# Entry 0's scores ahead of its values, and the other entries' projections in pieces of four row tiles, in a two-layer graph attention kernel

## The chip, the cores and the metric

The kernel runs on one core of one Trainium2 chip. The metric is the device time of one execution in microseconds (us); lower is better. A core has TensorE (PE, matrix products into PSUM), VectorE (DVE), ScalarE (ACT), GpSimd (POOL), and SyncE (SP), which here only issues DMA transfers. Data on the chip lie in SBUF.

## The reference

Eight graphs ("entries", B = 8) of N = 2048 nodes with D = 256 features share one adjacency matrix. Layer 0 is an attention layer of H = 8 heads of 32 features, layer 1 one with dot products as scores. After each there is a residual and a layer norm.

```python
# layer 0
x_proj = einsum('bnd,hdf->bhnf', x, W)
e_src  = einsum('bhnf,hf->bhn', x_proj, a_src)
e_dst  = einsum('bhnf,hf->bhn', x_proj, a_dst)
e = leaky_relu(e_src[..., :, None] + e_dst[..., None, :], 0.2)
e = e + softplus(beta_tilde) * log(adj + 1e-6)
e = where(adj > 0, e, neg_inf)
h = einsum('bhij,bhjf->bhif', softmax(e), x_proj)
x = layernorm(x + concat_heads(h) @ W_out.T)
# layer 1
h1, h2, h3 = x @ W1, x @ W2, x @ W3
e = where(adj > 0, leaky_relu(h1 @ h2.T, 0.2), NEG_INF)
x = layernorm(x + relu(softmax(e) @ h3))
```

## The kernel before, in words

All arithmetic is fp32. Rows of N are cut into NT = 16 row tiles of 128, or into NB = 4 groups of four row tiles (512 rows). D is two halves of 128 (KC = 2).

Layer 0 of an entry has two parts. The **projection** (`project`) transposes x on PE a group at a time (`turn`, L252; `tr` into PSUM, copied by ACT to `xt`, L257). It then multiplies each row tile by `wp`, the 256 columns of W and, behind them, 16 columns that give both score vectors of the eight heads (L267). ACT copies the values to `v` (L269) and the scores to `both` (L270). After the last row tile come the factors: the maximum over the tiles on DVE (L276) and over the partitions on POOL (L277), `cs` and the shifted scores (L279, L281), two exponents into `re`, and one DVE instruction that scales all of `v` (L286). Entries 1 to 7 then store `v` and `re` in device memory (`v_d`, `re_d`, L289). At last PE transposes `cs` (`est`, L293) and its exponent goes to `c_d` (L296), from where `query_rows` (L308) later reads each head's row back into all 128 partitions, as `c`.

The **attention** (`step`) makes 64 steps: four passes over two heads each (`hp`), and in a pass 16 tiles of source nodes (`jt`). A step needs the tile `mt` of the transposed mask weights. For each of the two heads DVE computes `s = max(c, re) * mt` (L330, 128x2048), and PE multiplies s into the numerator `val` and the denominator `den` (L355, 16 instructions each). The denominators of some tiles don't go over PE one by one: for the tiles in `SUMMED` (L67), ACT makes a scaled copy `d` of the first (L343), DVE adds the others to it (L337), and PE takes up the sum once with a product by ones at the pass's end. `finish` copies `val` and `den` out of PSUM and takes the reciprocals through device memory (`rc`, `rec_d`, `rb`). After every second pass DVE multiplies `ht` by them (L383).

The first pass of entry 0 makes the mask as well: `make_m` loads a block of adj (L176) and computes `m` (DVE L178 and L181, ACT L179 and L180). `make_mt` transposes it on PE (`mtp`, L190), copies it by ACT (L191) and stores it (`mt_d`, L192). Later passes load `mt` (L197).

`output` (products `y`, L408, and the first layer norm), `turn` (L424) and `Dot` are layer 1. From entry 1 on, layer 0 of entry b is woven into layer 1 of entry b - 1.

What sets the order: PE runs its instructions in the order in which the program writes them (L86). The order of the other engines and of the DMA queue on SP is fixed when the kernel is built, by a planner that takes instructions by their place in the program and by its estimate of when they can start. Each engine and SP then runs its own list in order. A tile's buffer count (`bufs`) says how many of a tag can live at once: four `s`, three PSUM tiles of the tag `mm`, one x group `xg` (L166).

Entry 0 is projected whole before its first step. The projections of entries 1 to 7 are cut into pieces, one row tile each with two more per entry for the factors and the `est` (7 x 18 = 126), and these are spread evenly over the first 60 of entry 0's steps:

```python
    pieces = (B - 1) * (NT + 2)
    for k in range(NP * NT):
        gats[0].step()
        due = [min(i * pieces // (NP * NT - 4), pieces) for i in (k, k + 1)]
        for _ in range(due[1] - due[0]):
            next(others)
```

In a piece that begins a group, the turn of the group after it comes just behind that row tile, and takes its x from a load that was issued when the turn before it was done. `later_weights` prepares the weights of the later stages in five further pieces. Entry 1's `v`, like that of all later entries, comes back from device memory (`load`, L301) into the tag `v`, which entry 0's values hold until its last step. The hand-over runs two steps of entry 1, two groups of entry 0's output, one step, two groups, one step (L547).

Of the kernel before, what the change touches and what calls it, by code (L numbers as in the profile page):

```python
# [9 lines left out]
F32 = mybir.dt.float32  # L10
BF16 = mybir.dt.bfloat16
I32 = mybir.dt.int32
AF = mybir.ActivationFunctionType
# [5 lines left out]
P = 128  # L19
# [8 lines left out]
def kernel(  # L28
# [35 lines left out]
    NP = H // HP  # L64
    IG = BK // P

    SUMMED = [(1, 3, 6, 8, 11, 13), (1, 3, 6, 9, 12)] + [(1, 3, 6, 8, 11, 13)] * (B - 2)  # L67

    const = ctx.enter_context(tc.tile_pool(name="const", bufs=1))
    dram = ctx.enter_context(tc.tile_pool(name="dram", bufs=1, space=DRAM))  # L70
# [7 lines left out]
    def mm_tile(name):  # L78
        return ps.tile([P, BK], F32, tag="mm", name=name)
# [25 lines left out]
    beta_c = beta[:, 3:4]  # L105


    first_x = [wide.tile([P, NT // 2, D], F32, tag="p", name="xr", bufs=2) for _ in range(2)]
    for half, xr in enumerate(first_x):
        nc.sync.dma_start(xr, x[0].rearrange("(t p) d -> p t d", p=P)[:, ts(half, NT // 2), :])  # L110


    wp = const.tile([P, KC, D + 2 * H], F32)
    for kc in range(KC):
        nc.sync.dma_start(
# [3 lines left out]
    for a, dst in ((a_dst, wp[:, :, D:D + H]), (a_src, wp[:, :, D + H:])):  # L119
        a_bc = small.tile([P, D], F32, tag="row", name="a_bc", bufs=4)  # L120
        nc.sync.dma_start(a_bc, bass.AP(tensor=a.tensor, offset=a.offset, ap=[[0, P], [1, D]]))
        for kc in range(KC):
            wa = small.tile([P, D], F32, tag="row", name="wa", bufs=4)
            nc.vector.tensor_mul(wa, wp[:, kc, 0:D], a_bc)
            nc.vector.tensor_reduce(dst[:, kc, :], wa.rearrange("p (h f) -> p h f", h=H), AX.X, ALU.add)  # L125

    wot = const.tile([P, KC, D], F32)
    w12 = const.tile([P, KC, D], F32)
# [30 lines left out]
    rec_d = dram.tile([B, NP, 4, HALF], F32, name="rec_d")  # L159
    x1_d = dram.tile([B, N, D], F32, name="x1_d")  # L160

    def x_groups():

        for b in range(1, B):
            for g in range(NB):
                xg = wide.tile([P, IG, D], F32, tag="pen", name="xg", bufs=1)  # L166
                nc.sync.dma_start(xg, x[b].rearrange("(t p) d -> p t d", p=P)[:, ts(g, IG), :])
                yield xg

    groups = x_groups()  # L170
    ahead = []

    def make_m(jt):

# [9 lines left out]
    def make_mt(jt, m):  # L184

        mt = wide_tile("mt", "mt", 2)
        for g in range(NB):
            t = mm_tile("mtp")
            for k in range(IG):
                nc.tensor.transpose(t[:, ts(k, P)], m[:, g * IG + k, :], ident)  # L190
            nc.scalar.copy(mt[:, ts(g, BK)], t)  # L191
        nc.sync.dma_start(mt_d[ts(jt, P), :], mt)  # L192
        return mt
# [36 lines left out]
    class Gat:  # L230
# [4 lines left out]
            self.units = ((hp, jt) for hp in range(NP) for jt in range(NT))  # L235
            self.ms, self.mts = [], []

        def project(self):


            b = self.b
            kept = "v" if b == 0 else ("h3", "x1t")[b % 2]
            self.v = v = whole.tile([P, NT, D], F32, tag=kept, name="v")
            both = small.tile([P, NT, 2 * H], F32, name="both", bufs=1)
            xts = []

            def turn(g):
                if b == 0:
                    xr = first_x[g // 2][:, ds(g % 2 * IG, IG), :]
                else:  # L250
                    xr = ahead.pop() if ahead else next(groups)
                xt = chunk.tile([P, KC, BK], F32, tag="ht", name="xt", bufs=3)  # L252
                for kc in range(KC):
                    t = mm_tile("tr")
                    for k in range(IG):
                        nc.tensor.transpose(t[:, ts(k, P)], xr[:, k, ts(kc, P)], ident)
                    nc.scalar.copy(xt[:, kc, :], t)  # L257
                xts.append(xt)
                if b > 0:
                    ahead.extend(xg for xg in [next(groups, None)] if xg is not None)  # L260

            turn(0)
            for it in range(NT):
                g, k = divmod(it, IG)
                t = mm_tile("proj")
                for kc in range(KC):
                    nc.tensor.matmul(t[:, 0:D + 2 * H], xts[g][:, kc, ts(k, P)], wp[:, kc, :],  # L267
                                     start=(kc == 0), stop=(kc == KC - 1))
                nc.scalar.copy(v[:, it, :], t[:, 0:D])  # L269
                nc.scalar.copy(both[:, it, :], t[:, D:D + 2 * H])  # L270
                if k == 0 and g + 1 < NB:
                    turn(g + 1)
                yield
            top = small.tile([P, 2, H], F32, name="top", bufs=1)
            ed, es = both[:, :, 0:H], both[:, :, H:2 * H]
            nc.vector.tensor_reduce(top[:, 0, :], ed.rearrange("p t h -> p h t"), AX.X, ALU.max)  # L276
            nc.gpsimd.partition_all_reduce(top[:, 1, :], top[:, 0, :], P, bass_isa.ReduceOp.max)  # L277
            cs = small.tile([P, H, NT], F32, name="cs", bufs=1)
            nc.vector.tensor_tensor(cs, es.rearrange("p t h -> p h t"),  # L279
                                    top[:, 1, :].unsqueeze(2).to_broadcast([P, H, NT]), ALU.add)  # L280
            nc.vector.tensor_tensor(ed, ed, top[:, 1:2, :].to_broadcast([P, NT, H]), ALU.subtract)  # L281
            self.re = re = small.tile([P, 2, NT, H], F32, name="re", bufs=2)
            nc.scalar.activation(re[:, 0], ed, AF.Exp, scale=-(1.0 - ALPHA))
            nc.scalar.activation(re[:, 1], ed, AF.Exp)
            v4 = v.rearrange("p t (h f) -> p (t h) f", f=DH)
            nc.vector.tensor_tensor(v4, v4, re[:, 1].rearrange("p t h -> p (t h)").unsqueeze(2).to_broadcast(  # L286
                [P, NT * H, DH]), ALU.mult)
            if b > 0:
                nc.sync.dma_start(v_d[b], v)  # L289
                nc.sync.dma_start(re_d[b], re)  # L290
            yield
            t = mm_tile("est")
            nc.tensor.transpose(t[:, 0:P], cs.rearrange("p h t -> p (h t)"), ident)  # L293
            est = row_tile("est")[:, 0:P]
            nc.scalar.activation(est, t[:, 0:P], AF.Exp, scale=1.0 - ALPHA)
            nc.sync.dma_start(c_d[b].rearrange("h (t p) -> (h t) p", p=P), est)  # L296
            yield

        def load(self):
            self.v = whole.tile([P, NT, D], F32, name="v")  # L300
# [4 lines left out]
        def query_rows(self, h):  # L305
# [2 lines left out]
            nc.sync.dma_start(c, c_d[self.b, h:h + 1, :].to_broadcast([P, N]))  # L308
            return c

        def step(self, count=1):

            for _ in range(count):
# [3 lines left out]
                    self.val = pacc.tile([P, HALF], F32, tag="val", name="val")  # L317
                    self.den = pacc.tile([P, HALF], F32, tag="den", name="den")
                first = self.b == 0 and hp == 0
                while first and len(self.mts) < min(jt + 2, NT):  # L320
                    at = len(self.mts)
                    while len(self.ms) < min(at + 1 + (jt > 0), NT):
                        self.ms.append(make_m(len(self.ms)))
                    self.mts.append(make_mt(at, self.ms[at]))
                mt = self.mts[jt] if first else load_mt(jt, self.b == 0)
                s = []
                for a in range(HP):
# [3 lines left out]
                    s.append(sa)  # L331
                v, e = self.v, self.re[:, 1]
                heads = [hp * HP + a for a in range(HP)]
                chain = () if first else SUMMED[self.b]
                if jt - 1 in chain[1:]:
                    for d, sa, h in zip(self.sums, self.last, heads):
                        nc.vector.scalar_tensor_tensor(d, sa, e[:, jt - 1, h:h + 1], d, ALU.mult, ALU.add)  # L337
                self.last = s
                self.products(self.val, [v[:, jt, ts(h, DH)] for h in heads], s, jt == 0, jt == NT - 1)
                if jt in chain[:1]:  # L340
                    self.sums = [wide_tile("d", "d" if self.b else "p", 2) for _ in heads]
                    for d, sa, h in zip(self.sums, s, heads):
                        nc.scalar.activation(d, sa, AF.Copy, scale=e[:, jt, h:h + 1])  # L343
                if jt not in chain:
# [170 lines left out]


    gats = [Gat(b) for b in range(B)]
    for _ in gats[0].project():
        pass
    others = (1 for g in gats[1:] for _ in g.project())  # L520
    weights = later_weights()
    pieces = (B - 1) * (NT + 2)
    for k in range(NP * NT):
        gats[0].step()
        due = [min(i * pieces // (NP * NT - 4), pieces) for i in (k, k + 1)]
        for _ in range(due[1] - due[0]):
            next(others)
        if k >= NT and k % 4 == 2:
            next(weights, None)

    dot = None
    for b in range(1, B + 1):
        gat, fresh = gats[b - 1], gats[b] if b < B else None

        def layer_0(count):
            if fresh:
                fresh.step(count)

        if fresh:
            fresh.load()  # L540
        rows = gat.output()

        def output(count):
            for _ in range(count):
                next(rows)

        if dot is None:  # L547
            layer_0(2)
            for _ in range(2):
                output(2)  # L550
                layer_0(1)
        else:

            dot.step(lambda k: layer_0((0, 0, 2)[k]))
            dot.step(lambda k: (output((1, 1, 2)[k]), layer_0((0, 1, 1)[k])))
        for _ in gat.turn():
            layer_0(1)
        dot = Dot(gat)
        dot.step(lambda k: layer_0((2, 1, 1)[k]))
        for i in range(NT - 3):  # L560
            dot.step(lambda k: layer_0((0, 2 - (i % 3 == 2), 2)[k]))
# [33 lines left out]
```

## Time and profile before

| | |
|---|---|
| time, median of 3 runs | 4466.91 us (4461.9 to 4466.94) |
| the profiled execution | 4464.3 us, span 4462.5 us |
| PE busy | 4254.7 us (95%) |
| DVE busy | 3688.7 us (83%) |
| ACT busy | 1682.0 us (38%) |
| moved by DMA | 843.53 MB, 189 GB/s over the span |
| `s` (L330) on DVE | 1024 instructions, 2342 ns each |
| `d` (L337) on DVE | 302 instructions, 2344 ns each |

How to read it: the profile is of one execution, and all its times are from the start of the span. "Busy" is the time in which an engine had an instruction running. The ends of matrix products are modelled, so PE's busy time is an upper reading. A group line names the line of the kernel, engine, operation, output and inputs, count, busy time and mean, and then the idle time of that engine just before the group and what ended it. A line of waits names who waited for whom: us in total, how many times, the longest. A timeline row has start, length, engine, line, operation, tiles and count, and in brackets the idle time before it with what ended that.

### The profile page before, as it was taken

The numbers are of one execution on the slowest core, as the hardware profiler recorded it, in microseconds if no ns is written. First come the engines' busy times: TensorE is split into PE (matmuls) and PEld (weight loads), VectorE is DVE, ScalarE is ACT, GpSimd is POOL, SyncE is SP. The second block draws the span as 40 slices with busy tenths as digits, with TensorE's granted clock in tenths as the row PEclk, the third lists the DMA queues.
The fourth block names the chain that finished last, engine by engine and source line by source line (L and its number), as shares of the span: only waits on it lengthen the run. The fifth ranks groups of instructions, "written<-read, shape, count | busy, mean of one in ns | idle before, by whom it ended". The sixth has DMA issues, their size and how long they took to land.

```text
span 4462.5 us, 59194 instructions
## 1 busy us (share of the span) xinstructions
PE 4254.7 (95%) x24748; PEld 2217.8 (50%) x24748; DVE 3688.7 (83%) x2603; ACT 1682.0 (38%) x3041; POOL 13.4 (0%) x14
## 2 busy tenths in 40 slices
PE   6888889999999999999999999999999999999999
PEld 4444344444454454545455454545444454444666
DVE  5799988898899889898989889898889979898222
ACT  5622223333333333333233333333233343333455
POOL 0000000000000000000000000000000000000000
PEclk9999899999999999999999999999999999999999
DMA  7877666666555565555545565555555564554211
GB/s 211 265 251 258 221 212 214 219 221 239 183 182 179 187 216 181 194 186 201 198 167 191 190 213 187 186 193 192 187 180 199 184 217 175 193 181 144 72 50 41
DMA packets 251501, 843.53 MB, mean 189 GB/s; under 512 B 32352, under 2 KB 151136, under 8 KB 175712
## 3 DMA queue, kind: packets, MB, share of 16 engines
q1 hardware_dynamic: 215904, 806.17, 51.7%
q10 hardware_dynamic: 35328, 33.56, 2.2%
q8 instruction: 194, 3.18, 0.3%
q14 instruction: 75, 0.61, 0.0%
HBM read 763.76 MB, written 75.37 MB: 188 GB/s over the span
## 4 chain that ended last, share of the span: by engine, by line
PE 60%; DVE 14%; issue 7%; DMA 3%; ACT 2%; SPq 0%; ACTq 0%; DVEq 0%
PE acc L504 16%; PE e L469 15%; PE val L355 12%; DVE s L330 9%; PE den L355 8%; PE pt L488 4%; DVE d L337 4%; DMA mt<-mt_d 2%; PE y L408 2%; PE h1p L459 2%; PE h3p L439 1%; DVE p L474 0%; ACT p L475 0%; DMA rc<-dn 0%; DVE ht L410 0%
## 5 line engine op out<-in xcount | busy, mean ns | idle before, releaser
L330 DVE SCALAR_TENSOR_TENSOR s<-c,re,mt 128x2048 f32<-128x2048 f32 x1024 | 2354.2, 2342 | 178.8 <-PE den L355 117.7
L355 PE MATMUL val<-s,v 128*32 128x512 f32 x8192 | 1044.2, 611 | 83.3 <-DVE s L330 79.2
L504 PE MATMUL acc<-h,pts 128*128 128x256 f32 x4096 | 949.6, 380 | 2.0 <-ACT pts L490 1.2
L469 PE MATMUL e<-x1t,h 128*128 128x512 f32 x2048 | 906.1, 595 | 6.6 <-ACT h L461 6.5
L504 PEld LDWEIGHTS acc<-h,pts 128*128 128x128 f32 x4096 | 748.2, 190 | 92.2 <-ACT pts L490 6.3
L337 DVE SCALAR_TENSOR_TENSOR d<-s,re,d 128x2048 f32<-128x2048 f32 x302 | 701.7, 2344 | 0.0
L355 PE MATMUL den<-s,re 128*32 128x512 f32 x5280 | 677.6, 602 | 3.2 <-ACT dn L370 3.2
L469 PEld LDWEIGHTS e<-x1t,h 128*128 128x128 f32 x2048 | 379.1, 190 | 459.3 <-issue 416.3
L355 PEld LDWEIGHTS val<-s,v 128*32 128x32 f32 x8192 | 244.4, 111 | 698.2 <-issue 507.4
L490 ACT COPY pts<-pt 128x512 f32<-128x512 f32 x512 | 298.7, 584 | 766.3 <-PE pt L488 759.1
L471 ACT ACTIVATE p<-e 128x512 f32<-128x512 f32 x512 | 303.4, 596 | 434.7 <-PE e L469 431.1
L474 DVE CUSTOM_DVE_ANT_0 p<-p,pen 128x2048 f32<-128x2048 f32 x128 | 293.0, 2289 | 203.8 <-ACT p L471 203.0
L355 PEld LDWEIGHTS den<-s,re 128*32 128x32 f32 x5280 | 186.6, 112 | 413.7 <-issue 399.3
L488 PEld LDWEIGHTS pt<-ident,p 128*128 128x128 f32 x2048 | 238.9, 141 | 222.8 <-issue 159.4
L475 ACT ACTIVATE p<-p,neg 128x2048 f32<-128x2048 f32 x128 | 256.9, 2007 | 239.7 <-DVE neg L474 239.7
L488 PE MATMUL pt<-ident,p 128*128 128x128 f32 x2048 | 319.3, 279 | 6.2 <-ACT p L475 6.2
L511 ACT ACTIVATE z<-acc,rec 128x256 f32<-128x256 f32 x128 | 60.9, 476 | 369.6 <-PE acc L504 339.7
L512 DVE TENSOR_TENSOR z<-z,x1r 128x256 f32<-128x256 f32 x128 | 53.8, 420 | 159.6 <-ACT z L511 156.1
L267 PE MATMUL proj<-wp,xt 128*128 128x272 f32 x512 | 142.0, 419 | 11.8 <-DVE wp L125 8.0
L439 PE MATMUL h3p<-w3s,x1t 128*128 128x256 f32 x512 | 124.0, 386 | 17.1 <-ACT x1t L434 16.2
L343 ACT ACTIVATE d<-s,re 128x2048 f32<-128x2048 f32 x62 | 124.3, 2008 | 35.4 <-DVE ht L383 24.6
L408 PE MATMUL y<-wot,ht 128*128 128x256 f32 x512 | 119.4, 390 | 15.8 <-DVE ht L383 15.8
(82 smaller groups left out, 1886.9 us busy)
## 6 DMA issues: line engine op xcount, KB each, us to landing
mt<-mt_d SPq DMA_DIRECT2D x496, 1024.0 KB, 4.9
c<-c_d SPq DMA_DIRECT2D x64, 1024.0 KB, 7.1
pen<-pen_d SPq DMA_DIRECT2D x112, 512.0 KB, 3.4
xg<-in_x_dram SPq DMA_DIRECT2D x60, 512.0 KB, 5.1
adj_t<-in_adj_dram SPq DMA_DIRECT2D x16, 1024.0 KB, 7.2
mt_d<-mt SPq DMA_DIRECT2D x16, 1024.0 KB, 8.3
rb<-rec_d SPq DMA_DIRECT2D x64, 256.0 KB, 4.2
x_d<-ht ACTq DMA_DIRECT2D x32, 512.0 KB, 3.6
```

The source lines that it names most:

```text
L330: nc.vector.scalar_tensor_tensor(sa, self.cs[a], self.re[:, 0, jt, h:h + 1], mt, ALU.max, ALU.mult)
L337: nc.vector.scalar_tensor_tensor(d, sa, e[:, jt - 1, h:h + 1], d, ALU.mult, ALU.add)
L355: nc.tensor.matmul(dst[ts(q, DH), ts(c, BK)], weights[q % 2], s[q % 2][:, ds(q // 2 * HALF + c * BK, BK)], start=start, stop=stop)
L408: nc.tensor.matmul(y[:, i, :], self.ht[:, g * IG + k + i, kc, :], wot[:, kc, :], start=(kc == 0), stop=(kc == KC - 1))
L439: nc.tensor.matmul(t[:, ts(i, D)], x1t[:, kc, ts(2 * (j - 1) + i, P)], w3s[:, kc, :], start=(kc == 0), stop=(kc == KC - 1))
L469: nc.tensor.matmul(t, self.h1[:, kc, ts(it % IG, P)], self.x1t[:, kc, ts(c, BK)], start=(kc == 0), stop=(kc == KC - 1))
L471: nc.scalar.activation(p[:, ts(c, BK)], t, AF.Prelu, alpha=ALPHA)
L474: nc.vector.tensor_tensor_reduce(p, p, pen, -1.0, FMAX, ALU.add, ALU.min, neg)
L475: nc.scalar.activation(p, p, AF.Exp, bias=neg, scale=-1.0, accum_out=den)
L488: nc.tensor.transpose(t[:, ts(k, P)], p[:, ts(g * IG + k, P)], ident)
L490: nc.scalar.copy(pt, t)
L504: nc.tensor.matmul(acc, now[:, ts(k, P)], self.h3[:, j, :], start=(j == 0), stop=(j == NT - 1))
```

## The change

Entry 0's x is loaded in four pieces of four row tiles, issued behind the weights. All its groups are transposed first, into one tile `xt0`. Then 64 small PE instructions compute the scores of all 16 row tiles at once (16 columns each, into one PSUM tile), the factors follow, and only then the values are computed, without the score columns, group by group, with the scaling of `v` cut into four pieces. The `est` of entry 0 comes after the first group, its first `mt` after the second.

The other entries' projections come as 28 pieces of four row tiles (one group), one on each second step (k = 1, 3, ...). A piece transposes the x of the piece after it first and asks for the x of the one after that; then it computes its own four row tiles, scores included. The `est` of an entry comes behind the first row tiles of the next one. The entries come in the order 2 to 7, then 1. Their values lie alternately in the tags `v` and `h3`; entry 1's stay in `v` and are neither stored nor loaded again, and entry 0's own lie in the tag `x1t`. Entry 0 sends all denominators over PE. The hand-over runs three steps of entry 1, all four groups of output, one step.

```diff
-    SUMMED = [(1, 3, 6, 8, 11, 13), (1, 3, 6, 9, 12)] + [(1, 3, 6, 8, 11, 13)] * (B - 2)
+    SUMMED = [(), (1, 3, 6, 9, 12)] + [(1, 3, 6, 8, 11, 13)] * (B - 2)
...
-            kept = "v" if b == 0 else ("h3", "x1t")[b % 2]
-            both = small.tile([P, NT, 2 * H], F32, name="both", bufs=1)
+            self.both = small.tile([P, NT, 2 * H], F32, name="both", bufs=2)
...
+        def scores_first(self, xt):
+            t = mm_tile("both")
+            for it in range(NT):
                 for kc in range(KC):
+                    nc.tensor.matmul(t[:, ts(it, 2 * H)], xt[:, kc, ts(it, P)], wp[:, kc, D:],
+                                     start=(kc == 0), stop=(kc == KC - 1))
+            nc.scalar.copy(self.both.rearrange("p t h -> p (t h)"), t[:, 0:NT * 2 * H])
...
+        def scale(self, g):
+            v = self.v[:, ts(g, IG), :].rearrange("p t (h f) -> p (t h) f", f=DH)
+            e = self.re[:, 1, ts(g, IG), :].rearrange("p t h -> p (t h)")
+            nc.vector.tensor_tensor(v, v, e.unsqueeze(2).to_broadcast([P, IG * H, DH]), ALU.mult)
...
-                while first and len(self.mts) < min(jt + 2, NT):
-                    at = len(self.mts)
-                    while len(self.ms) < min(at + 1 + (jt > 0), NT):
-                        self.ms.append(make_m(len(self.ms)))
-                    self.mts.append(make_mt(at, self.ms[at]))
+                if first:
+                    self.more_mt(jt + 2, jt > 0)
...
-                chain = () if first else SUMMED[self.b]
+                chain = SUMMED[self.b]
...
+    g0.begin("x1t")
+    xt0 = whole.tile([P, KC, N], F32, tag="heads", name="xt0")
+    for g in range(NB):
+        transpose_x(first_x[g // 2][:, ts(g % 2, IG), :], xt0[:, :, ts(g, BK)])
+    g0.scores_first(xt0)
+    g0.factors()
+    for g in range(NB):
+        g0.rows(g, xt0[:, :, ts(g, BK)], False)
+        g0.scale(g)
+        if g == 0:
+            g0.queries()
+        elif g == 1:
+            g0.more_mt(1)
...
+        items = [(gat, g) for gat in gats[2:] + gats[1:2] for g in range(NB)]
...
+        load(0)
+        turn(0)
+        for n, (gat, g) in enumerate(items):
+            turn(n + 1)
+            if g == 0:
+                gat.begin(("v", "h3")[n // NB % 2])
+            gat.rows(g, xts[n])
+            if g == 0 and n > 0:
+                items[n - 1][0].queries()
+            if g == NB - 1:
+                gat.factors()
+                for k in range(NB):
+                    gat.scale(k)
+                if gat.b > 1:
+                    gat.store()
+            yield
+        gats[1].queries()
+        yield
...
     for k in range(NP * NT):
-        gats[0].step()
-        due = [min(i * pieces // (NP * NT - 4), pieces) for i in (k, k + 1)]
-        for _ in range(due[1] - due[0]):
-            next(others)
-        if k >= NT and k % 4 == 2:
-            next(weights, None)
+        g0.step()
+        if k % 2 == 1:
+            next(pieces[0], None)
+            if k > NT and k % 4 == 1:
+                next(pieces[1], None)
...
-        if fresh:
+        if b > 1 and fresh:
             fresh.load()
...
-            layer_0(2)
-            for _ in range(2):
-                output(2)
-                layer_0(1)
+            layer_0(3)
+            output(4)
+            layer_0(1)
```

Here `more_mt` is the loop that `step` held before, `turn(n)` transposes the x of piece n and then issues the load of piece n + 1, and `store` holds the two stores of L289 and L290.

## The prediction

> **What bounds the kernel now.** I read the page first, then busy time by stage, then the waits and the timeline of the first 600 us. The page's slices (one is 112 us):
>
> ```profile
> PE   6888889999999999999999999999999999999999
> DVE  5799988898899889898989889898889979898222
> PEclk9999899999999999999999999999999999999999
> ```
>
> From the seventh slice on TensorE (PE) is busy throughout, and what the diff touches is over by then: entry 0's projection, its loop of 64 steps (four passes of 16), and the hand-over to entry 1. In the timeline of VectorE (DVE) the first `s` of the four passes starts at 56, 212, 325 and 439 us and entry 0's last `s` ends at 552. So I asked for busy time in these stretches (columns: stretch, length, PE, PEld, DVE, ACT, POOL, granted clock, DMA share, GB/s):
>
> ```profile
> 0.00:56.00 56.00, 28.06 (x129) 22.76 (x129) 17.91 (x24) 29.70 (x61) 1.07 (x7) 0.96 0.63 180
> 56.00:212.00 156.00, 135.10 (x920) 72.28 (x921) 122.83 (x63) 101.65 (x162) 0.36 (x1) 0.89 0.80 253
> 212.00:325.00 113.00, 92.25 (x572) 42.35 (x571) 105.91 (x52) 28.33 (x85) 4.63 (x2) 0.91 0.72 255
> 325.00:439.00 114.00, 100.34 (x627) 47.82 (x625) 108.15 (x53) 31.37 (x91) 2.69 (x2) 0.96 0.70 255
> 439.00:552.00 113.00, 93.03 (x574) 38.39 (x578) 106.34 (x52) 24.37 (x69) 4.63 (x2) 0.89 0.63 224
> 552.00:584.00 32.00, 15.90 (x98) 4.73 (x91) 16.72 (x9) 5.64 (x5) 0.00 (x0) 0.71 0.80 265
> ```
>
> Passes 1 to 3 (rows 3 to 5) are bound by DVE: 94 to 95% busy. Pass 0 is bound by nobody for long; the hand-over (last row) is mostly waiting. The waits of PE and of the DMA queue SP up to 580 us, and three moments:
>
> ```profile
> PE val L355 <- DVE s L330: 35.3, 20, 8.1
> PE tr L256 <- DMA xg<-in_x_dram: 24.3, 7, 5.9
> PE est L293 <- DVE cs L279: 15.4, 5, 4.1
> SPq L197 <- DVE s L330: 117.5, 30, 8.6
> ...
> 55.95 2.35 DVE L330 SCALAR_TENSOR_TENSOR s<-c,re,mt 128x2048 f32<-128x2048 f32 x1 [3.90 <-DMA c<-c_d]
> 576.44 4.61 DVE L330 SCALAR_TENSOR_TENSOR s<-c,re,mt 128x2048 f32<-128x2048 f32 x2 [11.80 <-DMA mt<-mt_d]
> 583.31 1.22 PE L408 MATMUL y<-wot,ht 128*128 128x256 f32 x2 [12.22 <-DVE ht L383]
> ```
>
> Seven times, once per entry, PE waits for the next x, because the turn of the second group follows one row tile after the first. Five times it waits for `cs`. Such a stall holds back products and `mtp` transposes, so DVE starves as well (10.7 us at 69 to 80, 10.2 at 160 to 170).
>
> **What the Trainium skill says.** "TensorE: Matmul & The Clock Gate", Part 1: after an idle window of about 3.4 us the array runs at half clock. The trace agrees: the granted clock is 0.50 in 56 to 66 us, after 8 us of waiting, and 0.71 in the hand-over, but 0.99 once PE is dense. "DMA: Bandwidth & Descriptors", Anatomy of one DMA: a semaphore wait happens on the issuing sequencer before dispatch. The trace agrees: SP is held up to 8.6 us by an `mt` load whose buffer is in use, and what stands behind it on SP waits too.
>
> **The change part by part.** Prices are start-to-start spacings at full clock in this trace: one `s` or `d` 2.26 us on DVE; the 16 instructions of `val`, or of `den`, 1.72 on PE; a transpose 0.109; a projection instruction 0.229, 16 of them for four row tiles.
>
> *Start (0 to 56).* The weights are issued ahead of x. The wait for them ended at 19.9 us before; x, now behind some 12 us of weight issue on SP, lands at about 14 to 20. Then 32 transposes at half clock (0.213 each, 6.8 us), held by x until about 22. New are 64 score instructions of 16 columns, which no row of before shows. Low end: their weight loads alone, 128 columns/1.2 = 107 ns by the TensorE page's LDWEIGHTS section, 6.8 us. High end: the 0.229 of a projection instruction, 14.7 us. I take 9, nearer the low end, since the trace's transposes load such weights every 0.109. So scores end at 31. Maximum, POOL reduction, `cs` and exponents took 2.3 us before (43.2 to 45.5) and now run beside the first four row tiles (16 x 0.216 = 3.5 us). The `est` transpose stands behind those, so `c_d` is issued at about 36.5; from its issue to the first `s` it took 55.95 - 45.5 = 10.4 us. First `s` at 47, bounds 43 to 54: -9. The other three row groups and `mt` 0 (12 us of PE) and the scaling, now four pieces of about 1.15 us for one of 4.42, lie beside these two DMAs. The 16 columns and 16 small ACT copies that the rows lose are under 1 us.
>
> *Pass 0 (156).* DVE: 32 x 2.26 = 72.4; mask work 12 x 1.14 + 14 x 2.20 = 44.5; two entries' maxima and scalings 2 x 5.3 = 10.6; sum 127.5. PE: 16 x 3.43 + 14 x 1.74 + 8 pieces x (8 x 0.109 + 16 x 0.229 = 4.54) = 115.6. DMA: 39.4 MB plus one more `v` store, 41.5, at 253/0.80 = 316 GB/s at best: 131. One x wait stays (the second piece's x is asked for just before it is needed, 4.7 us); the other goes. DVE's sum, this wait, 4 us for `c` at the border and 6 for coupling of four nearly full engines: 142, bounds 133 to 156. -14.
>
> *Passes 1 and 2 (113 + 114).* Ten `d` per pass leave DVE (22.6 us); two scalings of 2 us leave ACT, which had time. PE gets six `den` groups less the closing one, 5 x 1.72 = 8.6. DVE: 72.4 + 10.6 + 1 = 84. PE: 54.9 + 8 x 4.54 = 91.2, at clock 0.96 95. So PE becomes the bound. Steps of 3.43 and 7.97 us in turn on PE, against 4.53 on DVE, fit in the four `s` buffers, which let DVE be two steps ahead. The border of a pass (`c`, PSUM) stays: 4 us. 99 each, bounds 95 to 106: -29 together. DMA: 27.3 MB in 99 us = 276 GB/s against 255/0.72 = 354: share 0.78, no bound.
>
> *Pass 3 (113).* Four pieces by step 55, the last `est` at 57. Eight steps 27.4 + 18.2 = 45.6 on PE, /0.96 = 47.5; eight bound by DVE, 8 x 4.53 = 36.2; border 3: 87, bounds 82 to 95. -26.
>
> *Hand-over.* Entry 1's `v` is neither stored nor loaded: 4 MB and two SP issues less, and PE's 3.9 us wait for it goes. From the last `den` (559.5) to the `y` row above (583.3) were 23.8 us; the chain without the `mt` wait is `dn` 1.1, `rc` 3.7, reciprocal 0.4, `rec_d` 3.5, `rb` 5, `ht` 2.3 = 16. Three steps instead of two now fill it (10.3 us of PE). -7 for the chain, -3.4 for the step moved in: -10, bounds -3 to -14. Four output groups in a row, instead of two and two, take a step's filler out from between; that is inside these bounds.
>
> Later stages are PE-bound and only move earlier. PE's net extra work (15 x 1.72 + 9 - 1 = 34 us) is in the sums.
>
> Sum: -9 - 14 - 29 - 26 - 10 = -88 on the span of 4462.5. That execution took 4464.3 and the three timed runs have their median at 4466.9; I keep the difference: 4466.9 - 88 = 4379. All good ends give -13 - 23 - 37 - 31 - 14 = -118 (4349), all bad ends -2 - 0 - 15 - 18 - 3 = -38 (4429).
>
> **The rivals.** *Half the gain.* Pass 0 is held by DMA (share already 0.97 in 106 to 116 us) and by ACT, which has to evict four row tiles in a burst through three PSUM buffers between exponents of 2 us; pass 1 meets the same bursts. For it: ACT is busy 84 to 91% of 96 to 136 us. Against: PE has about 0.9 us of slack per step there. The bad ends: 4429.
> *Slower: x queued behind `mt` on SP.* There is one x buffer; its load is issued after the transposes that free it and must get past `mt` loads that wait for DVE. A piece comes every 11 us, so x (4.7 us to landing) can be held about 6 us before PE waits; PE being the bound, each further us counts. 28 pieces with more than 88/28 = 3.1 us of wait undo the gain; if each waited the full 4.7, 132 - 88 = +44: 4511. Against: SP was held 8.6 us at the longest, and 3.9 on average.
> *No change:* PE takes over one for one. That needs passes of 113 us on PE, a clock of 0.81; the lowest pass had 0.89 with stalls in it. 4467.
>
> **How the numbers follow.** The main case 0.71, half the gain 0.19 (faster too), slower 0.07, no change 0.03. 0.2% (9 us) is about what a measurement of this kernel can tell from none. The range 4349 to 4429 takes all good and all bad ends; outside are slower, none and a little below.
>
> **What would show it.** Right: no `d` (L337) before entry 1; first `s` at 43 to 54; passes of about 142, 99, 99, 87; PE busier than DVE in passes 1 and 2, at clock 0.95 or more; the x wait once rather than seven times; the `cs` wait nearly gone; no `v_d` load at the hand-over and its chain at 16 us. Wrong: DVE still over 93% busy in passes 1 and 2, PE waiting for x more than thrice, a first `s` after 56, or stages after 700 us that became longer.

## The result, and the profile after

| | before | after |
|---|---|---|
| time, median | 4466.9 us (4461.9 to 4471.2, 4 runs) | 4388.1 us (4386.2 to 4391.9, 4 runs) |
| ratio | | 0.9825 [0.9808, 0.9842] |
| the profiled execution | 4464.3 us, span 4462.5 | 4391.9 us, span 4389.8 |
| `d` on DVE | 302 | 272 |

The change takes 78.8 us off; 88 were forecast. The two profiled spans differ by 72.7 us, and the accounts below are made against these. The slices of the changed kernel (one is 110 us):

```profile
PE   7899899999999999999999999999999999999999
DVE  6888888998989898997989988898889889898222
PEclk9999999999999999999999999999999999999999
```

Of the slices 2 to 6 three now show PE at 9, where all were at 8, and the clock is at 9 in every slice. Cut at the first `s` of each pass, which are now at 41.0, 193.5, 292.9, 390.9 and, for entry 1, 485.6 us (columns as in the prediction's table of stretches):

```profile
0.00:41.00 41.00, 28.00 (x151) 25.05 (x152) 13.50 (x22) 18.96 (x32) 1.08 (x7) 0.88 0.66 195
41.00:193.50 152.50, 130.84 (x927) 75.28 (x925) 127.88 (x70) 108.07 (x171) 1.18 (x1) 0.96 0.88 277
193.50:293.00 99.50, 97.94 (x720) 48.40 (x724) 84.11 (x49) 28.87 (x95) 2.69 (x2) 1.00 0.79 289
293.00:391.00 98.00, 96.89 (x718) 48.55 (x714) 86.28 (x49) 27.86 (x91) 0.73 (x2) 1.00 0.80 297
391.00:486.00 95.00, 85.13 (x632) 34.76 (x628) 84.29 (x48) 17.56 (x57) 0.73 (x2) 0.96 0.64 233
486.00:516.00 30.00, 18.04 (x112) 4.05 (x104) 22.14 (x11) 5.03 (x4) 0.00 (x0) 0.86 0.68 230
```

Passes 1 and 2 (rows 3 and 4) are bound by PE, busy for 98.4 and 98.9% at clock 1.00; DVE's work in them fell from 105.9 and 108.2 to 84.1 and 86.3. Pass 0 (row 2) still has no engine full, and in pass 3 (row 5) PE and DVE take turns. The waits of PE from 41 to 486 us, and of SP in entry 0:

```profile
PE val L361 <- DVE s L336: 18.4, 13, 5.7
PE tr L172 <- DMA xg<-in_x_dram: 4.6, 2, 4.1
PE mtp L192 <- ACT mt L193: 6.8, 7, 1.4
PE mtp L192 <- DVE m L183: 4.1, 1, 4.1
...
SPq L199 <- DVE s L336: 102.8, 26, 7.6
```

PE waits for x twice rather than seven times (4.6 us for 24.3), and not at all for `cs`. SP's longest stand behind `mt` is 7.6 us (8.6 before).

| stage, us | before | after | forecast | measured |
|---|---|---|---|---|
| start, to the first `s` | 56.0 | 41.0 | -9 | -15.0 |
| pass 0 | 155.9 | 152.5 | -14 | -3.4 |
| passes 1 and 2 | 227.0 | 197.4 | -29 | -29.6 |
| pass 3 | 112.6 | 94.7 | -26 | -17.9 |
| hand-over, to the first `s` of entry 1's second pass | 130.7 | 122.8 | -10 | -7.9 |
| later | | | 0 | +1.1 |
| sum | | | -88 | -72.7 |

The middle of the forecast stood; its two ends, pass 0 and pass 3, gave 18.7 us less, and the start gave 6 more.

### The profile page after: what moved, and what is told of

The parts are those of the page before. It is cut to its first block, busy times and chain, and to the rows that moved or that the text cites. A ratio compares the mean times of both kernels' runs of the same rounds, so it can differ in the third digit from the quotient of the medians.

```text
span 4389.8 us, 59761 instructions
## 1 busy us (share of the span) xinstructions
PE 4243.0 (97%) x25052; PEld 2226.0 (51%) x25052; DVE 3624.5 (83%) x2597; ACT 1666.5 (38%) x3020; POOL 6.4 (0%) x14
## 4 chain that ended last, share of the span: by engine, by line
PE 56%; DVE 18%; issue 9%; DMA 4%; ACT 2%; SPq 1%; ACTq 0%; DVEq 0%
PE acc L510 15%; PE e L475 14%; DVE s L336 11%; PE val L361 11%; PE den L361 7%; DVE d L343 4%; PE pt L494 4%; DMA mt<-mt_d 3%; PE y L414 2%; PE h1p L465 2%; PE h3p L445 1%; DVE p L480 1%; ACT p L481 1%; DMA rc<-dn 1%; SPq L379 0%
## 5 line engine op out<-in xcount | busy, mean ns | idle before, releaser
L361 PE MATMUL val<-s,v 128*32 128x512 f32 x8192 | 1030.0, 604 | 67.8 <-DVE s L336 67.3
L361 PE MATMUL den<-s,re 128*32 128x512 f32 x5568 | 709.0, 599 | 3.3 <-ACT dn L376 3.3
L343 DVE SCALAR_TENSOR_TENSOR d<-s,re,d 128x2048 f32<-128x2048 f32 x272 | 632.2, 2344 | 0.0
L480 DVE CUSTOM_DVE_ANT_0 p<-p,pen 128x2048 f32<-128x2048 f32 x128 | 292.9, 2288 | 198.2 <-ACT p L477 197.5
L518 DVE TENSOR_TENSOR z<-z,x1r 128x256 f32<-128x256 f32 x128 | 53.8, 421 | 156.1 <-ACT z L517 155.9
L262 PE MATMUL proj<-wp,xt 128*128 128x272 f32 (+1 forms) x512 | 125.5, 398 | 0.1
L349 ACT ACTIVATE d<-s,re 128x2048 f32<-128x2048 f32 x56 | 112.1, 2005 | 29.1 <-DMA mt<-mt_d 23.5
```

The source lines that it names most:

```text
L361: nc.tensor.matmul(dst[ts(q, DH), ts(c, BK)], weights[q % 2], s[q % 2][:, ds(q // 2 * HALF + c * BK, BK)], start=start, stop=stop)
L480: nc.vector.tensor_tensor_reduce(p, p, pen, -1.0, FMAX, ALU.add, ALU.min, neg)
```

## The experiments

Four sets ran, each with the kernel before on the same chip; its medians there were 4465.1, 4466.0, 4467.0 and 4463.8 us. All gains below are against the one of the same set. The changed kernel itself was run a second time, as `a_repeat`:

> The kernel after itself, on the same chip as the next one: 4388, first s between 41 and 45 us (it differed by 3.6 us between runs with the same start), passes 152, 99, 98 and 95.

It took 4394.1 us (4390.3 to 4396.7), ratio 0.9841 [0.9828, 0.9855]: a gain of 69.7 us against 78.8 the first time, with the first `s` at 43.6 and passes of 152.8, 99.5, 98.3 and 94.6. So gains of different sets that lie within some 9 us of each other say nothing; what follows rests on stage lengths and on kernels of one set.

### Which part shortens passes 1 to 3

*`b_nochain`:* the kernel before, with entry 0's denominators all over PE.

```diff
-    SUMMED = [(1, 3, 6, 8, 11, 13), (1, 3, 6, 9, 12)] + ...
+    SUMMED = [(), (1, 3, 6, 9, 12)] + ...
```

> The kernel before with one edit: entry 0 sends all denominators over PE. Account held so far: DVE's work in passes 1 to 3 falls to about 84 us each, PE's rises to 89 us at full clock, but PE keeps its waits for x and for cs (some 10 us a pass), so a pass takes about 104 instead of 113 us, all three some 315, and the time is 4440 (4432 to 4448). Rival, that the relief of DVE is the whole gain: passes near 98, 4421. Rival, that PE takes over one for one: no change.

4443.1 us (4439.8 to 4443.7), ratio 0.9948 [0.9932, 0.9965], -22.0. Two of its passes (1 and 2), and its waits of PE:

```profile
213.00:323.70 110.70, 97.97 (x660) 43.22 (x660) 84.23 (x42) 23.45 (x80) 2.68 (x2) 0.91 0.70 257
323.70:429.20 105.50, 97.67 (x699) 45.04 (x700) 86.29 (x43) 26.12 (x85) 2.68 (x2) 0.98 0.78 280
...
PE tr L256 <- DMA xg<-in_x_dram: 21.7, 7, 4.3
PE est L293 <- DVE cs L279: 11.0, 7, 4.6
```

DVE has as little work as in the changed kernel (84.2 and 86.3 us), but passes 1 and 2 take 110.7 and 105.5 us rather than 99.4 and 98.0 (about 104 were expected), since PE still waits for x and `cs`. The time is the expected one (4432 to 4448).

*`a_chain`:* the changed kernel, with entry 0's sums back on DVE in passes 1 to 3.

```diff
-    SUMMED = [(), (1, 3, 6, 9, 12)] + ...
+    SUMMED = [(1, 3, 6, 8, 11, 13), (1, 3, 6, 9, 12)] + ...
-                chain = SUMMED[self.b]
+                chain = () if first else SUMMED[self.b]
-                    self.sums = [wide_tile("d", "d", 2) for _ in heads]
+                    self.sums = [wide_tile("d", "d" if self.b else "p", 2) for _ in heads]
```

> The kernel after with one edit: in passes 1 to 3 of entry 0 six of 16 denominators go over DVE and ACT again, as before. Account held so far: DVE has 107 us of work per pass, becomes the bound again, passes take about 110 instead of 99, 98 and 95, and the time rises by 37 to 4425 (4415 to 4435). Rival, that the pieces and the early x made the gain: passes stay near 100, 4390.

4436.3 us (4433.8 to 4439.2), ratio 0.9936 [0.9921, 0.995], -28.8. Passes 1 and 2, and the first of its waits of PE:

```profile
198.90:310.50 111.60, 96.79 (x622) 45.78 (x622) 106.42 (x58) 32.66 (x97) 4.63 (x2) 0.95 0.71 252
310.50:424.30 113.80, 97.17 (x634) 46.07 (x634) 108.82 (x59) 31.34 (x93) 2.68 (x2) 0.97 0.72 258
...
PE val L361 <- DVE s L336: 62.3, 39, 7.4
```

DVE is back at 95% of the pass, and PE waits for `s` 39 times. The pieces of four row tiles gain almost nothing while DVE is full. Passes 1 and 2 came out 2 to 4 us longer than expected, the total 11; some 5 us of that lie ahead of pass 1 (first `s` at 43.6, pass 0 of 155.3 us).

*`a_weave`:* the changed kernel, with its other projections cut and spread as before: one row tile a piece, 126 pieces over 60 steps, the turn behind the first row tile of a group, the `est` in a piece of its own behind the factors. The pieces of the later weights stand at their old steps too.

```diff
-            turn(n + 1)
-            gat.rows(g, xts[n])
-            if g == 0 and n > 0:
-                items[n - 1][0].queries()
+            for k in range(IG):
+                gat.row(g, k, xts[n])
+                if k == 0 and g + 1 < NB:
+                    turn(n + 1)
+                yield
...
-        if k % 2 == 1:
+        due = [min(i * 126 // (NP * NT - 4), 126) for i in (k, k + 1)]
+        for _ in range(due[1] - due[0]):
```

> The kernel after with the other entries' projections woven in as before: one row tile each, 126 pieces over 60 steps, the turn of the next group behind a group's first row tile, the est in a piece of its own right behind the factors. Entry order, tags and all else as after. Account held so far: seven waits for x of 3.5 us and the waits for cs of 15 us come back on PE, which is the bound now, and passes 1 and 2 take 105 to 110: 4418 (4408 to 4428). Rival, that the four s buffers hide these waits: at most 4396.

4419.6 us (4418.0 to 4429.7), ratio 0.9903 [0.9888, 0.9918], -45.5; passes of 155.8, 112.1, 105.6 and 105.0. Its waits of PE:

```profile
PE tr L172 <- DMA xg<-in_x_dram: 23.9, 7, 5.5
...
PE est L300 <- DVE cs L280: 7.8, 6, 4.6
```

The seven x waits are back with the weave, and so it is the new weave that takes them off. It differs in two things, the larger piece and the earlier turn; `a_halves` below halves the piece, keeps the early turn and waits for x only once (4.1 us), which speaks for the turn. The three runs belong together. Against the kernel before, the sums alone give 22.0 us, everything but the sums 28.8; that is 51 for both, and the whole change gives 70 to 79. Each part takes away one of two limits that lie close to one another (DVE's 106 us of work, PE's 92 plus its stalls), so each alone runs into the other. The weave is worth 24 to 33 of it.

*`a_halves`:* two row tiles on every step instead of four on each second.

```diff
-            gat.rows(g, xts[n])
+            gat.rows(g, xts[n], part=0)
+            yield
+            gat.rows(g, xts[n], part=1)
...
-        if k % 2 == 1:
+        if k > 0:
             next(pieces[0], None)
```

> The kernel after with each piece in two halves of two row tiles, one on every step from k = 1 on; the turn and the load stay with the first half. Account: passes 1 and 2 are bound by PE's sum of work, which is the same, so they stay at 97 to 100; in pass 0 the mtp transposes that free a mask buffer wait for a shorter burst, 0 to 4 us less; 4384 to 4388. Rival, that the size of the piece made the gain: passes over 103, 4400 or more.

4396.0 us (4391.5 to 4402.1), ratio 0.9842 [0.9827, 0.9857]. Passes of 150.5, 98.6, 105.3 and 94.6: as in the changed kernel but for pass 2, where one wait of DVE stands out in its timeline:

```profile
332.12 9.14 DVE L336 SCALAR_TENSOR_TENSOR s<-c,re,mt 128x2048 f32<-128x2048 f32 x4 [5.40 <-DMA mt<-mt_d]
```

On SP no `mt` load is issued between 304.7 and 325.8 us in this run; the loads of `rb`, the stores of `re` and `v`, the `c_d` store and two x loads stand between. This is the queue of the slower rival, with the roles changed (`mt` behind x and the stores), and it costs once. So the expected 4384 to 4388 was missed. Passes 1 and 3 are as short with half the piece, so the size of the piece is not what made them short.

### The start and pass 0

*`a_x_first`:* the changed kernel, with x issued ahead of the weights.

```diff
+    first_x = [wide.tile([P, NT // 2, D], F32, tag="p", name="xr", bufs=2) for _ in range(2)]
+    for g in range(NB):
+        nc.sync.dma_start(first_x[g // 2][:, ts(g % 2, IG), :], ...)
...
-    first_x = ...
-    for g in range(NB):
-        nc.sync.dma_start(first_x[g // 2][:, ts(g % 2, IG), :], ...)
```

> The kernel after with one edit: entry 0's four x loads are issued ahead of the weights, as before. Account: the weights then land late, as before (their products began at 19.9 us), so the scores start 4 us later and end near 30, and the first s comes at 45 to 49 instead of 41; as the mask chain paces the first steps, pass 1's first s is at most 4 us later than 193.5 and the time 4388 to 4392. Rival, that the start sets the end one for one: pass 1's first s at 198 to 201, 4394.

4393.7 us (4393.1 to 4398.2), ratio 0.9838 [0.9824, 0.9853]. The first `s` comes at 47.8 us; in the changed kernel and the runs that share its start it comes at 41.0 to 44.6. Pass 1 begins at 199.0 us, beside 193.5 and 196.4 in the two profiles of the changed kernel. So my account (at most 197.5) failed and the rival (198 to 201) held: a later start moves the end of pass 0 nearly one for one. The total, -72.3, lies between the two of the changed kernel, so only the stages show it. The issue of `wp` and the scores, here:

```profile
3.28 4.12 SPq L115 DMA_DIRECT2D wp<-in_L_gnn_W_dram  x2
20.32 13.81 PE L251 MATMUL both<-wp,xt 128*128 128x16 f32 x64 [3.76 <-DVE wp L125]
...
20.30:34.20 13.90, 13.88 (x65) 13.90 (x66) 3.63 (x3) 2.66 (x3) 0.00 (x0) 0.50 0.51 142
```

and in the changed kernel:

```profile
1.16 1.04 SPq L110 DMA_DIRECT2D wp<-in_L_gnn_W_dram  x2
9.92 4.43 PE L172 MATMUL tr<-ident,xr 128*128 128x128 f32 x24 [9.92 <-DMA xr<-in_x_dram]
15.72 10.18 PE L251 MATMUL both<-wp,xt 128*128 128x16 f32 x64
18.31 1.23 DVE L180 TENSOR_SCALAR m<-adj_t 128x2048 f32<-128x2048 int32 x1 [5.23 <-issue]
25.94 0.37 ACT L253 COPY both<-both 128x256 f32<-128x256 f32 x1 [9.38 <-PE both L251]
28.10 2.01 ACT L181 ACTIVATE m<-m,eps_prior 128x2048 f32<-128x2048 f32 x1
41.03 4.61 DVE L336 SCALAR_TENSOR_TENSOR s<-c,re,mt 128x2048 f32<-128x2048 f32 x2
...
15.70:25.90 10.20, 10.20 (x67) 10.20 (x66) 1.23 (x1) 0.86 (x2) 0.00 (x0) 0.69 0.72 193
18.00:19.00 1.00, 1.00 (x12) 1.00 (x11) 0.69 (x1) 0.00 (x0) 0.00 (x0) 1.00 1.22 292
20.00:21.00 1.00, 1.00 (x6) 1.00 (x7) 0.00 (x0) 0.00 (x0) 0.00 (x0) 0.50 1.11 333
```

The same two DMAs for `wp` hold SP for 1.04 us when they come first and 4.12 behind x. The 64 score instructions took 10.18 us at a mean clock of 0.69 and 13.81 at 0.50: 7.0 and 6.9 us of full clock, about 0.11 each. That is the low end of the bound that I took from the Trainium skill ("TensorE: Matmul & The Clock Gate", LDWEIGHTS): loading 128 columns of weights sets their pace (PEld is busy all the time), and the rest is the clock.

Part 1 of that page puts half clock after an idle window of about 3.4 us; in `a_x_first` the clock fell at 19.0 us, 2.5 us into the 3.76 us of waiting ahead of the scores, which agrees roughly. But waiting does not explain the rest. There the clock stayed at 0.50 through all 13.81 us of the scores. In the changed kernel no wait of more than 0.5 us stands close ahead of the scores: they began at full clock (the row from 18 us), and at 19.6 us, in the midst of them and with PE busy without a break, it fell to 0.50 (the row from 20 us). It was back at 29.8, 4.1 us after the next products, of 256 columns, had begun. All eleven profiles of kernels with the weights issued ahead of x show such a fall, 2.5 to 5.5 us after the first score. So a full row of PE in the profile does not mean a full clock. That the few columns are the cause fits these times, but no run here has other widths.

The rows also show what pass 0 suffers from. From 16.5 to 25.9 ACT stands idle (9.38) in front of the copy of the scores. Mask 0's logarithm (L181) is ready at 19.5, when the DVE instruction before it ends, but is queued behind that copy.

*`a_masks_first`:* the masks 0 and 1 are traced ahead of the scores, and ACT's part of the score path is queued behind mask 0's exponent.

```diff
+    for jt in range(2):
+        g0.ms.append(make_m(jt))
+    with tc.issue_after(exps[0].ins):
-    g0.scores_first(xt0)
+        g0.scores_first(xt0)
...
```

> The kernel after with one edit at the start: masks 0 and 1 come ahead of the scores in the program, and ACT's copies of scores and values are queued behind mask 0's two exponent steps. In the profile of after ACT idles from 16.5 to 25.9 us with mask 0's first step ready at 19.5, and pass 0 began 15 us earlier but gained only 3.5 us more. Account held: pass 0 is paced by the chain of masks (adj load, DVE, ACT twice, DVE, PE, ACT), which this starts 8 us earlier, so pass 1's first s comes at about 187 instead of 193.5 and the time is 4382. Rival, that pass 0 is at its DMA floor (share 0.88): pass 1's first s stays at 192 to 194 and the time at 4388.

4386.3 us (4382.7 to 4389.9), ratio 0.9823 [0.9809, 0.9838]. Mask 0 is done at 26.3 us (36.2 in the changed kernel), the first `s` comes at 42.4, pass 1 begins at 190.3: about half of the way from 193.5 to the 187 of my theory. The rest goes into the wait for the second piece's x:

```profile
67.23 1.17 PE L172 MATMUL tr<-ident,xg 128*128 128x128 f32 x8 [4.15 <-DMA xg<-in_x_dram]
75.46 1.23 DVE L182 TENSOR_SCALAR m<-adj_t 128x2048 f32<-128x2048 int32 x1 [8.98 <-PE mtp L194]
```

A stop of 4.15 us on PE leaves DVE idle for 8.98. In the changed kernel the same place has 4.12 and 6.60:

```profile
71.27 1.94 PE L172 MATMUL tr<-ident,xg 128*128 128x128 f32 x8 [4.12 <-DMA xg<-in_x_dram]
79.22 1.23 DVE L180 TENSOR_SCALAR m<-adj_t 128x2048 f32<-128x2048 int32 x1 [6.60 <-PE mtp L192]
```

*`a_masks_x2`:* so the second piece's x too is loaded early, into a tile that is free then; this is added to `a_masks_first`.

```diff
+            if n == 1:
+                xgs.append(whole.tile([P, IG, D], F32, tag="h3", name="xh"))
+                nc.sync.dma_start(xgs[1], ...)
...
-                load(n + 1)
+                if n != 1:
+                    load(n + 1 + (n == 0))
...
         load(0)
+        load(1)
```

> The kernel with masks first (run before this) and one more edit: the x of the second piece is loaded at the start, into the tag h3 that is free until the fifth piece, and every later load goes out as before. In the run with masks first PE stood 4.15 us for this x in pass 0, and DVE 9.0 us behind it. If pass 0's missing gain is these start-up waits, pass 0 shortens by 4 us more, from 147.9 to 144, and the time is 4382. Rival, DMA floor (share 0.87): pass 0 stays at 147 to 149 and the time at 4386.

4384.4 us (4381.5 to 4386.0), ratio 0.9814 [0.98, 0.9827], -82.6; pass 0 is 143.6 us, as expected, and the other passes stay at 99.4, 98.0 and 93.5. So the rival, a floor set by DMA in pass 0 (147 to 149), did not hold. PE's waits for x are gone from its pass 0:

```profile
PE val L363 <- DVE s L338: 11.1, 3, 5.7
PE mtp L194 <- ACT mt L195: 5.4, 6, 1.2
```

### Pass 3

*`a_mx2_spread`:* as `a_masks_x2`, with the 28 pieces spread over 60 steps rather than 55, to take some of PE's work out of pass 1 and the last factors out of the DVE-bound end.

```diff
-        if k % 2 == 1:
+        if k < 60 and (k + 1) * 28 // 60 > k * 28 // 60 or k == 61:
             next(pieces[0], None)
```

> The kernel with masks first and the second x early, and the 28 pieces spread evenly over 60 steps instead of every second one up to step 55. In the profile of after PE is the bound up to step 55, and DVE in the last eight steps, where the last entry's factors (5.6 us on DVE) fall too. Moving about two pieces of 4.5 us of PE from passes 1 and 2 behind step 55 makes these 2 us shorter each and leaves pass 3 as it is: 4378 to 4380. Rival, that an uneven distance of the pieces meets late mt loads or full s buffers, as the halves did: 4384 or more.

4388.7 us (4386.0 to 4391.2), ratio 0.9825 [0.9811, 0.9838]: no gain over `a_masks_x2`, rather 4.3 us more. Passes 1 and 3, and the first `s` of pass 1:

```profile
190.00:285.50 95.50, 91.82 (x666) 45.11 (x670) 83.78 (x48) 23.08 (x82) 0.73 (x2) 0.98 0.76 266
383.10:482.20 99.10, 93.37 (x674) 43.35 (x674) 84.00 (x48) 23.28 (x77) 0.73 (x2) 0.98 0.66 239
...
189.97 6.88 DVE L338 SCALAR_TENSOR_TENSOR s<-c,re,mt 128x2048 f32<-128x2048 f32 x3 [8.47 <-DMA mt<-mt_d]
```

Pass 1 is 3.9 us shorter than in `a_masks_x2` and pass 3 is 5.6 longer: PE's work moves from one to the other. All three passes together are 1.3 us longer. In pass 3 DVE also waits longer for `c` (4.2 us, 0.8 in `a_masks_x2`); how much of the 5.6 is PE's work isn't shown. The larger part of the loss lies ahead of pass 1: pass 0 takes 146.6 us for 143.6, and at its end DVE waits 8.47 us for an `mt` load, where `a_masks_x2` waits 4.83 for ACT's copy of `mt`. My expectation failed, and the late `mt` load is what its rival named.

### The hand-over

*`a_v_trip`:* entry 1's values are stored and loaded again, as those of all others.

```diff
-    g0.begin("x1t")
+    g0.begin("v")
-                gat.begin(("v", "h3")[n // NB % 2])
+                gat.begin(("x1t", "h3")[n // NB % 2])
-                if gat.b > 1:
-                    gat.store()
+                gat.store()
-        if b > 1 and fresh:
+        if fresh:
```

> The kernel after with entry 1's values stored and loaded again as before: entry 0's values lie in the tag v, the others alternate in x1t and h3, all seven entries are stored, and entry 1's v is loaded when entry 0's last step frees the tag. Account held so far: PE waits 4 to 6 us for the load at the hand-over, and the mt loads stand behind 2 MB more: 4 to 10 us slower than after, 4392 to 4398, all of it between pass 3 and step 16 of entry 1. Rival, that the hand-over is set by the chain of reciprocals anyway: 4388.

4394.5 us (4392.8 to 4397.4), ratio 0.9838 [0.9822, 0.9854]. The wait is there:

```profile
498.12 3.64 PE L361 MATMUL val<-s,v 128*32 128x512 f32 x16 [6.38 <-DMA v<-v_d]
```

but the hand-over takes 125.6 us, beside 122.8 and 125.0 for the two profiles of the changed kernel. The time lies in the expected 4392 to 4398, but `a_repeat`, without this trip, took 4394.1. What the values that stay on the chip are worth is not established; in this stage it is at most some 3 us.

*`a_hand_212`:* the hand-over in the order of before.

```diff
-            layer_0(3)
-            output(4)
+            layer_0(2)
+            for _ in range(2):
+                output(2)
+                layer_0(1)
-            layer_0(1)
```

> The kernel after with the hand-over's order of before: two steps, two output groups, one step, two groups, one step. The prediction had it that the third step moved in front fills 3.4 us of PE's wait: 4391. Rival, from the profile of after, where the product with the reciprocals (L389) stands on DVE behind the s and d of the steps put in front and the first full y came 27.0 us after the copy of the denominators, against 23.7 before: the third step in front delays the output by as much as it fills, 4388 or a little less.

4387.5 us (4383.4 to 4390.1), ratio 0.9821 [0.9807, 0.9836], hand-over 121.3. The changed kernel's chain, from its timeline:

```profile
489.71 1.01 ACT L376 COPY dn<-den 128x1024 f32<-128x1024 f32 x1
509.86 2.35 DVE L336 SCALAR_TENSOR_TENSOR s<-c,re,mt 128x2048 f32<-128x2048 f32 x1 [2.30 <-PE den L361]
512.12 2.35 DVE L343 SCALAR_TENSOR_TENSOR d<-s,re,d 128x2048 f32<-128x2048 f32 x1
514.39 2.28 DVE L389 TENSOR_TENSOR ht<-ht,rb 128x2048 f32<-128x2048 f32 x1
516.73 15.90 PE L414 MATMUL y<-wot,ht 128*128 128x256 f32 x62 [6.29 <-DVE ht L389]
```

and the same `y` in `a_hand_212`:

```profile
513.40 6.85 PE L414 MATMUL y<-wot,ht 128*128 128x256 f32 x22 [12.28 <-DVE ht L389]
```

Three steps ahead of the output shorten PE's idle time from 12.28 to 6.29 us, but `ht` then stands on DVE behind one more `s`, which itself waits 2.30 us for a free buffer: from `dn` to `y` 27.0 us, in the order 2-2-1-2-1 22.1. One about pays for the other. In the stage the order of before is even the shorter one: 121.3 us here and 122.0 in `a_mx2_212`, beside 122.8, 125.0 and 124.6 with three steps ahead (the changed kernel twice, `a_masks_x2`). In the total these runs can't measure it.

### The best of them together

*`a_mx2_212`:* `a_masks_x2` with the hand-over of before (both diffs above).

> The kernel with masks first and the second x early, and the hand-over's order of before (two steps, two output groups, one step, two, one). If the third step in front delays the output by as much as it fills, as the run with that order alone showed (22.1 us from the copy of the denominators to the full y instead of 27.0, the time the same), this is 4383 to 4385; if the shorter chain counts once the rest is earlier, 4379 to 4381.

4383.4 us (4380.9 to 4387.5), ratio 0.9821 [0.9808, 0.9834] against the kernel before, -80.3. In the same set the changed kernel (`a_repeat`) took 4394.1: 10.6 us more, and the ranges don't overlap. Its pass 0, from a first `s` at 43.8:

```profile
43.80:187.90 144.10, 127.03 (x909) 70.06 (x907) 125.49 (x68) 103.26 (x166) 1.18 (x1) 0.96 0.88 280
```

Pass 0 takes 152.8 us in `a_repeat` and 144.1 here; passes 1 and 2 take 99.5 and 98 in both. Most of the 10.6 us is pass 0, and 3.0 are the hand-over (125.0 and 122.0). The time is the one expected for an order that is worth nothing (4383 to 4385).

## Why the prediction was right, step by step

*Passes 1 and 2* (-29, measured -29.6): right in mechanism; that the size is right too has luck in it. PE's work was put at 91.2 us a pass, at clock 0.96, with 4 us of border. PE was busy for 97.9 and 96.9 us at clock 1.00 and idle for 1.6 and 1.1. Of the missing work, 2.5 us in pass 1 are products for the later weights and `est` that the sum left out; the rest isn't shown. The new bound is PE, and `b_nochain`, `a_chain` and `a_weave` show that both parts are needed for it: without the sums' removal DVE binds again (112 and 114 us), without the new weave the x waits return (112 and 106). The rival "no change" needed a clock of 0.81; it was 1.00.

*Start* (-9, measured -15): the direction was right; the term mis-sized is the wait for x behind "some 12 us of weight issue on SP". I had read the length of these issues in the profile of before, where x stood ahead of them; issued first, `wp` took 1.04 us, and the transposes began at 9.9 us rather than about 14 to 20. `a_x_first` shows the backlog again (4.12). The scores came out at 10.2 us for my 9, near it by luck: their spacing was at my low end (7 us in all at full clock), and the half clock of the last 6 us added the rest.

*Pass 0* (-14, measured -3.4): the failed step is the sum "DVE's sum, this wait, 4 us for `c` and 6 for coupling". It is close to the sum of engine work but leaves out the chain of a mask (adj, DVE, ACT, DVE, PE, ACT), which the score path now delays on ACT: mask 0 was done at 36.2 us (32.7 before) although the first `s` came earlier. Two runs bear this out. With masks 0 and 1 ahead pass 0 fell to 147.9 (mask 0 alone is not it: in `a_x_first` mask 0 was done at 26.1 us, mask 1 only at 45.6, and pass 0 took 151.2), and with the x wait gone too to 143.6; I had counted that wait, 4.7 us, within my 142, so some 6 us of coupling remain that my sum lacks. The rival "half the gain" named this place and ACT; its other half, bursts in pass 1, did not come.

*Pass 3* (-26, measured -17.9): the failed step is "eight bound by DVE, 8 x 4.53 = 36.2". The timeline of DVE in the changed kernel:

```profile
440.52 9.14 DVE L336 SCALAR_TENSOR_TENSOR s<-c,re,mt 128x2048 f32<-128x2048 f32 x4 [2.56 <-PE den L361]
449.57 0.36 DVE L272 TENSOR_REDUCE top<-both 128x8 f32<-128x128 f32 x1
451.69 4.63 DVE L286 TENSOR_TENSOR v<-v,re 128x1024 f32<-128x1024 f32 x4 [0.62 <-ACT re L280]
456.24 9.13 DVE L336 SCALAR_TENSOR_TENSOR s<-c,re,mt 128x2048 f32<-128x2048 f32 x4
467.44 20.45 DVE L336 SCALAR_TENSOR_TENSOR s<-c,re,mt 128x2048 f32<-128x2048 f32 x9 [2.07 <-PE den L361]
```

DVE runs two steps ahead, so the factors of the last entry, written at step 55, fall among the `s` of the last eight steps: no `s` from 449.6 to 456.2, 6.6 us, and a wait of 2.07 for a full set of `s` buffers. Together 36.2 + 6.6 + 2.1 = 44.9; measured 45.1 (440.5 to 485.6). The eight steps before took 49.6 for 47.5. Whether the factors would be better elsewhere stays open: `a_mx2_spread` moved them only together with PE's work, and lost.

*Hand-over* (-10, measured -7.9, and -5.7 in `a_repeat`): the failed term is the chain of 16 us; it took 27.0 (23.8 before), since I had `ht` in it without what stands ahead of it on DVE. That PE has more to do meanwhile was right: its wait for `ht` fell from 12.2 to 6.3 us and that for `v` (3.9) is gone, while its waits for `s` in this stage grew from 1.4 to 7.2. `a_hand_212` shows that the third step in front gains nothing.

*The slower rival* had a mechanism that exists (the late `mt` in `a_halves`), but the changed kernel's x waits cost 4.6 us in all. A kernel with later loads of x, which would price them, was not run.

## What to carry to other kernels

When two engines that feed one another are both near full, take the work off one and the stalls off the other in one step: each alone gave 22 and 29 us here, the whole change 70 to 79. Sum the work by stage to find the new bound, but for a stage where no engine is full follow one item through its chain and see what each engine has queued ahead of it. An engine that runs steps ahead moves its side work by as many steps: look where that work lands, not where the program has it. And a stage can be slower than its work at full clock, with its engine busy throughout, so read the granted clock beside the busy share.

## What was unexpected of the hardware

The issue of the same two `wp` transfers held SP for 1.04, 4.12 and 6.16 us: first in the queue, behind four x loads, and in the kernel before. The length of an issue row is thus no property of the transfer.

PE's granted clock fell from 1.00 to 0.50 within the 64 score products of 16 columns, though PE was busy for all of their 10.2 us.

The same kernel's gain over the one before was 78.8 and 69.7 us in two sets, and its first `s` came between 41.0 and 44.6 us in runs with the same start. Of the 2.5 us between its own two profiles, 0.8 are a later begin of the scores and 1.3 their length (10.18 and 11.49 us): in one the clock fell 3.9 us after their begin, in the other 2.5.
